# One list of steps from the first product on: the first half-slot of a quantised gated layer joins the ordered list, and the loads and weight ranges ahead of it are rearranged

## The chip, the core and the metric

The kernel runs on one core of one Trainium2 chip. Five engines work side by side, each through its own queue in order: TensorE (PE), VectorE (DVE), ScalarE (ACT), GpSimd (POOL) and SyncE (SP), which here issues nearly all DMAs. The metric is the device time in microseconds (us), as the median of the runs.

## The reference

For x of 4 x 1024 x 512 numbers, a condition of 4 x 128, norm_w (512 x 128), up_w (4096 x 512) and down_w (512 x 2048):

```
scale = cond @ norm_w.T + 1.0
ms = mean(x * x, axis=-1)
h = x * (scale[:, None, :] * rsqrt(ms + 1e-6))
u = h @ up_w.T
val, gate = split(u, 2)
h = val * gelu(gate)
y = act_quant(h) @ weight_quant(down_w).T
return y + x
```

act_quant rounds each token's row to 255 levels of its largest value, weight_quant rounds down_w to -1, 0, 1 times its mean size.

## The kernel before

The work goes in four batches of 1024 tokens, one for each row of the condition. The up product is cut into 16 blocks j of 128 value rows and 128 gate rows of up_w (the W blocks: t = 0 is the value half, t = 1 the gate half). Each factor is carried as two float16 numbers, a high part and a low part, and a product of two such numbers is made as three matmuls (high times high, and the two mixed ones). W rows and tokens are first scaled by powers of two, so that the parts fit.

In the first batch W has to be brought into that form while it is used. A block is loaded (w_load, line 310), its largest value is found (w_largest, 322: for blocks 0 to 2 by a reduce on DVE, from block 3 on by a sum on ACT), a power of two is made of it (w_factor_steps, 335), the rows are scaled by it (w_scale, 373, on POOL for blocks 0 and 1), PE turns 128 x 128 tiles into PSUM (w_turn, 382), ACT copies the high part out (w_high, 417) and DVE subtracts it for the low part (w_low, 426). Blocks 0 to 4 are multiplied plainly, in halves of 512 tokens: the steps gate, gelu, value and out (759 to 776), each of gate and value being 12 matmuls; the blocks after them run as slots (801), in which seven products serve for eight, and their parts go through DRAM: s_high, s_low and s_spill write them out (457 to 478).

x of the first batch needs, for each of its 8 tiles of 128 tokens, a sum of squares (first_sum, 1142), a root on ACT and a Newton step of five small DVE instructions for each pair of tiles (rsqrt_root, 1149; rsqrt_steps, 1155), a scaling (first_scale, 1169), four turns on PE (first_turn, 1176), a high part on ACT (first_high, 1181) and a low part on DVE (first_low, 1185), both multiplied by the condition's scale. That scale comes from cond: a row of the condition is spread over the partitions by PE (cond_first_row, 210), multiplied with norm_w on DVE (cond_scale, 216), its largest value found (cond_largest, 222), turned, reduced, floored to a power of two (cond_range_steps, 237), spread again (cond_spread, 256) and divided out (cond_undo, 262). The other three rows' scales come from small PE products with the turned norm_w (cond_turn, 191; cond_scale_rest, 201).

The order is written out by hand, and every engine takes its part of it in that order. It has three pieces. The first (1122 to 1260) issues the loads and brings four x tiles and block 0 into form; products of zeros (keep_warm, 1191) keep PE busy meanwhile. The second, plain_first (778), makes the 24 matmuls of block 0 with the first 512 tokens; two groups of other steps are put in between (second_part, 1263, ahead of matmul 6, and second_slot, 1291, ahead of matmul 16). The third is FIRST_BATCH (1380), a string of step names that take (1375) looks up in STEPS (1337) and issues one by one: all that is left of the first batch. In a name such as gate.1.0 the numbers are the step's arguments, here block 1 and half 0; slot.5.14 is the fifteenth step of block 5's slot, its value sum (856). Later batches are ordered by a planner with costs, which the change leaves as it is.

PSUM has eight banks: A and E two each, B one, po three. A tile that takes a bank waits until the one before it there has been read.

Of the kernel before, what the change touches and what calls it, by code (L numbers as in the profile page):

```python
# [51 lines left out]
def glu_quant_kernel(  # L52
# [138 lines left out]
    def cond_turn():  # L191

        pt = bank("E", 2, name="pc_t")
        PE.transpose(pt[:, :B], cn, ident[:B, :B])
        ACT.copy(cT, pt[:, :B])
        pt = bank("E", 2, name="nw_t")
        for k in range(NK):
            PE.transpose(pt[:, k * P : (k + 1) * P], nw[:, k], ident)
        ACT.copy(nwT, pt)
# [62 lines left out]
    def cond_undo(pd, b0, b1):  # L262
        DVE.reciprocal(ux[:, b0:b1], pd)
        if b0 == 0:
            DVE.tensor_scalar(scT[:, :, 0], scT[:, :, 0], ux[:, 0:1], None, ALU.mult)
# [512 lines left out]
    def plain_first(between):  # L778

        ps = {1: bank("B", 1, name="pg_0_0"), 0: bank("A", 2, name="pv_0_0")}  # L780
        gate, a21, a22 = a_parts(0)
# [4 lines left out]
        for n, (t, w, l, k) in enumerate(order):
            if n in between:
                between[n]()
            a = [gate[:, 0], gate[:, 1]] if t else [a21, a22]
# [1 line left out]
            PE.matmul(  # L791
                ps[t], a[:, w, k % 2, :], XP[:, l, k, :TOK],
                start=w + l + k == 0, stop=l == 1 and k == NK - 1,
            )
# [360 lines left out]
    def rsqrt_steps(n, m, z):  # L1155

        t, y = ssq0[:, n : n + m], rs0[:, n : n + m]
        ms = sm.tile([P, m], F32, name=f"mean_sq_{n}", bufs=1)
        DVE.reciprocal(y, z)
# [809 lines left out]
```

## Time and profile before

| | us |
|---|---|
| median of 3 runs | 710.73 (709.88 to 711.68) |
| the profiled execution | 710.89 |
| its span in the profile | 709.0 |
| around the span | 1.89 |

| engine | busy us | share of the span |
|---|---|---|
| PE, matmuls | 702.5 | 99% |
| DVE | 594.8 | 84% |
| ACT | 397.1 | 56% |
| POOL | 152.5 | 22% |

A line of a timeline has the start and the duration of an instruction (or of several alike, as x5), the engine, the line of the kernel, the operation, the tile written and the tiles read, and in brackets how long the engine had stood idle and what released it. Times are from the start of the span. A line of the waits names who waited, for whom, how long in all, how often, and the longest. A line of a table by stretches has the stretch, its length, the busy time and the number of instructions of PE, PE's weight loads, DVE, ACT and POOL, the share of its clock that PE was granted, the share of the DMA engines, and GB/s.

### The profile page before, as it was taken

The numbers are of one execution on the slowest core, as the hardware profiler recorded it, in microseconds if no ns is written. First come the engines' busy times: TensorE is split into PE (matmuls) and PEld (weight loads), VectorE is DVE, ScalarE is ACT, GpSimd is POOL, SyncE is SP. The second block draws the span as 40 slices with busy tenths as digits, with TensorE's granted clock in tenths as the row PEclk, the third lists the DMA queues.
The fourth block names the chain that finished last, engine by engine and source line by source line (L and its number), as shares of the span: only waits on it lengthen the run. The fifth ranks groups of instructions, "written<-read, shape, count | busy, mean of one in ns | idle before, by whom it ended". The sixth has DMA issues, their size and how long they took to land.

```text
span 709.0 us, 10268 instructions
## 1 busy us (share of the span) xinstructions
PE 702.5 (99%) x3668; PEld 359.8 (51%) x3668; DVE 594.8 (84%) x888; ACT 397.1 (56%) x692; POOL 152.5 (22%) x162
## 2 busy tenths in 40 slices
...
GB/s 259 323 268 253 249 198 260 218 207 226 272 131 167 178 178 165 140 178 210 133 113 110 133 106 171 178 183 148 219 104 97 99 103 103 101 100 99 77 223 104
DMA packets 223188, 120.26 MB, mean 170 GB/s; under 512 B 185353, under 2 KB 194589, under 8 KB 223138
## 3 DMA queue, kind: packets, MB, share of 16 engines
...
q10 hardware_dynamic: 152, 0.13, 0.1%
...
## 4 chain that ended last, share of the span: by engine, by line
PE 97%; DVE 1%; ACT 1%; DMA 1%; issue 0%; ACTq 0%; SPq 0%
PE A L703 43%; PE E L703 21%; PE B L703 11%; PE po L1071 9%; PE pg L718 3%; PE pv L718 3%; PE po_end L1018 2%; PE po_n L1071 2%; PE pz L1195 1%; DMA s_dram<-s_rows 1%; PE ptx L1179 1%; PE pv L791 0%; PE po_B L1071 0%; PE pg L791 0%; PE pw L388 0%; PE po_A L1071 0%
## 5 line engine op out<-in xcount | busy, mean ns | idle before, releaser
L703 PEld LDWEIGHTS <-SXY 128*128 128x128 f16 x2268 | 221.7, 98 | 260.7
L703 PE MATMUL A<-R,SXY 128*128 128x512 f16 x1170 | 270.7, 379 | 0.0
L703 PE MATMUL E<-R,SXY 128*128 128x512 f16 x606 | 147.2, 379 | 0.0
L840 DVE SCALAR_TENSOR_TENSOR H<-A,sg,t 128x512 f32<-128x512 f32 x59 | 44.2, 749 | 59.7 <-PE A L703 56.9
L851 ACT ACTIVATE t<-t,sg 128x512 f32<-128x512 f32 x59 | 42.5, 720 | 68.1 <-DVE t L848 67.9
L703 PE MATMUL B<-R,SXY 128*128 128x512 f16 x324 | 78.8, 379 | 0.0
L993 DVE TENSOR_TENSOR H<-H,am 128x1024 f32<-128x1024 f32 (+1 forms) x64 | 76.9, 1221 | 1.2 <-POOL am L962 1.2
L911 DVE TENSOR_REDUCE gm<-H 128x512 f32<-128x1024 f32 x56 | 69.2, 1236 | 1.0
L827 ACT COPY t<-A 128x512 f32<-128x512 f32 x59 | 34.4, 583 | 57.1 <-PE A L703 56.1
L927 POOL PARTITION_ALL_REDUCE am<-R x8 | 14.3, 1793 | 221.3 <-DVE R L913 221.3
L834 ACT ACTIVATE t<-B,sg 128x512 f32<-128x512 f32 x59 | 40.5, 686 | 37.7 <-PE B L703 37.7
L1071 PEld LDWEIGHTS <-R 128*128 128x128 bf16 (+1 forms) x512 | 50.1, 98 | 10.1
L857 DVE TENSOR_TENSOR v<-A,v 128x512 f32<-128x512 f32 x59 | 40.4, 684 | 15.1 <-PE A L703 12.5
L820 ACT COPY v<-E 128x512 f32<-128x512 f32 x59 | 34.5, 585 | 32.3 <-PE E L703 30.2
L1071 PE MATMUL po<-wd,R 128*128 128x256 fp8e4 x416 | 52.4, 273 | 0.0
L812 ACT COPY B<-A 128x512 f32<-128x512 f32 x59 | 33.8, 573 | 32.8 <-PE A L703 32.2
L860 DVE SCALAR_TENSOR_TENSOR H<-v,sg,t 128x512 f32<-128x512 f32 x59 | 45.8, 777 | 7.1 <-ACT t L851 6.7
L848 DVE TENSOR_TENSOR t<-E,t 128x512 f32<-128x512 f32 x59 | 39.9, 679 | 6.6 <-PE E L703 6.6
L913 DVE TENSOR_TENSOR R<-R,gm 128x512 f32<-128x512 f32 x56 | 41.7, 745 | 1.1
L1001 ACT CAST R<-H 128x1024 bf16<-128x1024 int32 x38 | 39.1, 1045 | 6.0 <-DVE H L993 5.6
L578 POOL TENSOR_SCALAR ssq<-ssq 128x2 f32<-128x2 f32 x12 | 5.5, 454 | 164.1 <-ACT xt L608 116.1
L703 PEld LDWEIGHTS <-R 128*128 128x128 f16 x210 | 20.5, 98 | 25.6 <-issue 0.9
...
## 6 DMA issues: line engine op xcount, KB each, us to landing
...
```

Source lines behind the costliest of these rows:

```text
L703: PE.matmul(o, s[:, w, k, :], operand(g // NJ, c, l, k), start=start and n == 0, stop=stop and n == len(TERMS) - 1, skip_group_check=True,)
L718: PE.matmul(ps, a[k // 2][:, w, k % 2, :], XP[:, l, k, h * TOK : (h + 1) * TOK], start=n == 0, stop=n == len(terms) - 1,)
L834: ACT.activation(self.t1, self.B, AF.Gelu, scale=gain(self.g, 1))
L840: DVE.scalar_tensor_tensor(h_half(self.g, 0), self.A, gain(self.g, 0), self.t1, ALU.mult, ALU.mult)
L848: DVE.tensor_tensor(self.t2, self.E, self.t2, ALU.add)
L851: ACT.activation(self.t2, self.t2, AF.Gelu, scale=gain(self.g, 1))
L857: DVE.tensor_tensor(self.v, self.A, self.v, ALU.add)
L860: DVE.scalar_tensor_tensor(h_half(self.g, 1), self.v, gain(self.g, 0), self.t2, ALU.mult, ALU.mult)
L911: DVE.tensor_reduce(gm[0], v, AX.X, ALU.max, apply_absolute_value=True)
L913: return [largest, lambda: DVE.tensor_tensor(m, m, gm[0], ALU.max)]
L993: DVE.tensor_tensor(v.bitcast(I32) if whole else v, v, r.to_broadcast([P, 2, TOK]), ALU.mult)
L1071: PE.matmul(po, w[:, j], m, start=start and j == 0, stop=stop and j == n - 1, skip_group_check=True,)
```

## The change

The work is the same but for small things; its order and its engines change.

- **Loads on SP:** x 0:2, then norm_w, x 2:4, W0, W1, x 4:6, x 6:8, W2. Before: norm_w, x 0:2, x 2:4, W0, x 4:6, x 6:8, W1, W2.
- **Ahead of the first product:** eleven products of zeros instead of sixteen. The first pair of x tiles is scaled, and tile 0 turned, before the second pair is squared; norm_w is turned early, and its copy on ACT stands behind the second root. The condition's largest is clamped by a fifth column of 1e-30 instead of an instruction, and the factor 1/256 is in the row that spreads it.
- **W0 and W1 are ranged by sums of absolute values:** three halves on ACT (half_sum), the value half of W0 on DVE (value_sum), each half with its own factor.
- **W0's gate half** is copied and split in two quarter-size pieces on DVE (gate_half) instead of one copy on ACT and one subtraction on DVE.
- **plain_first, second_part and second_slot are gone.** Their matmuls, turns, splits, squares and scalings are steps of FIRST_BATCH; x4 is scaled on POOL, its square is on ACT. The gate product takes a bank A and the value product a bank E; before it was B and A.
- **The rest of FIRST_BATCH** holds the same steps as before in another order.

```diff
     DVE.memset(unmagic, -MAGIC)
-    one = cpool.tile([P, 1], F32, name="one")
+    one = cpool.tile([P, 2], F32, name="one")
+    one, down_x = one[:, 0:1], one[:, 1:2]
     DVE.memset(one, 1.0)
+    DVE.memset(down_x, 1.0 / X_UP)
...
-    scT = cpool.tile([P, NK, B], F32, name="scT")
+    scT5 = cpool.tile([P, NK + 1, B], F32, name="scT")
+    scT = scT5[:, :NK]
+    DVE.memset(scT5[:, NK], 1e-30)
...
-    def cond_turn():
-        pt = bank("E", 2, name="pc_t")
+    def cond_turn(pt):
...
         ACT.copy(cT, pt[:, :B])
-        pt = bank("E", 2, name="nw_t")
+    def weight_turn(pt):
...
             PE.transpose(pt[:, k * P : (k + 1) * P], nw[:, k], ident)
+    def weight_copy(pt):
...
     def cond_largest(b0, b1):
-        v = scT[:, :, b0:b1]
         if b0 == 0:
+            v = scT[:, :, b0:b1]
             DVE.tensor_scalar(v, v, 1.0, None, ALU.add)
+        v = scT5[:, :, b0:b1]
...
         yield
-        DVE.tensor_scalar(d4, d4, 1e-30, None, ALU.max)
-        yield
...
         DVE.tensor_scalar(dg, ident[:n, :n], d4, 1.0 / X_UP, ALU.mult, ALU.mult)
+    def cond_range_one(pm):
+        d1 = sm.tile([B, 1], F32, name="d4_0", tag="d4")[:1]
+        DVE.tensor_reduce(d1, pm, AX.X, ALU.max)
+        yield d1
+        pow2_floor(d1)
+    def cond_undo_steps(pd):
+        DVE.reciprocal(ux[:, 0:1], pd)
+        yield
+        DVE.tensor_scalar(scT[:, :, 0], scT[:, :, 0], ux[:, 0:1], None, ALU.mult)
+        yield
+        DVE.tensor_copy(dx[:, 0:1], pd)
...
         DVE.reciprocal(ux[:, b0:b1], pd)
-        if b0 == 0:
-            DVE.tensor_scalar(scT[:, :, 0], scT[:, :, 0], ux[:, 0:1], None, ALU.mult)
...
         return am
+    def half_sum(j, t):
+        am = sm.tile([P, 2], F32, name=f"wam_{j}_{t}", tag="wam")[:, t : t + 1]
+        jk = junk[:, 2 * j].bitcast(F16)[:, :D]
+        ACT.activation(jk, wn(j)[:, t], AF.Abs, scale=0.5 / W_UP, accum_out=am)
+        return am
+    def value_sum():
+        am = sm.tile([P, 2], F32, name="wam_0_0", tag="wam")[:, 0:1]
+        DVE.tensor_reduce(am, wn(0)[:, 0], AX.X, ALU.add, apply_absolute_value=True)
+        return am
+    def half_factor_steps(j, t, am, u=1.0):
+        c = slice(t, t + 1)
+        pow2_floor(am)
+        yield
+        DVE.tensor_scalar(sw[:, j, c], am, u, 0.5 * 2.0**-100 / W_UP, ALU.mult, ALU.max)
+        yield
+        if j not in iv:
+            iv[j] = sm.tile([P, 2], F32, name=f"iv_{j}", tag="iv", bufs=3)
+        DVE.reciprocal(iv[j][:, c], sw[:, j, c])
...
             ACT.copy(a22[:, 0], v[:, 1])
+    def gate_half(n):
+        gate, _, _ = a_parts(0)
+        g = pw[0][0][:, n * HALF : (n + 1) * HALF]
+        DVE.tensor_copy(gate[:, n, 0], g)
+        DVE.tensor_tensor(gate[:, n, 1], g, gate[:, n, 0], ALU.subtract)
...
-    def plain_first(between):
...
+    PLAIN = [(1, w, 0, k) for w in range(2) for k in range(2)]
+    PLAIN += [(1, w, 0, k) for k in range(2, NK) for w in range(2)]
+    PLAIN += [(0, w, 0, k) for w in range(2) for k in range(NK)]
+    PLAIN += [(t, 0, 1, k) for k in range(NK) for t in (1, 0)]
+    def first_product(n):
+        t, w, l, k = PLAIN[n]
+        if w + l + k == 0:
+            halves[0, 0, t] = bank("A" if t else "E", 2, name=f"{'vg'[t]}_0_0")
         gate, a21, a22 = a_parts(0)
+        a = ([gate[:, 0], gate[:, 1]] if t else [a21, a22])[k // 2]
+        a = a.rearrange("p w (k f) -> p w k f", k=2)
+        PE.matmul(
+            halves[0, 0, t], a[:, w, k % 2, :], XP[:, l, k, :TOK],
+            start=w + l + k == 0, stop=l == 1 and k == NK - 1,
+        )
+    def first_gelu():
+        halves[0, 0] = wpool.tile([P, TOK], F32, name="g_0_0", tag="t1")
+        ACT.activation(halves[0, 0], halves[0, 0, 1], AF.Gelu, scale=gain(0, 1))
+    def first_out():
+        DVE.scalar_tensor_tensor(
+            h_half(0, 0), halves[0, 0, 0], gain(0, 0), halves[0, 0], ALU.mult, ALU.mult
+        )
...
     ACT.dma_start(out=cn, in_=cond)
-    SP.dma_start(out=nw, in_=norm_w.rearrange("(k p) c -> p k c", p=P))
-    ACT.activation(start_t, one, AF.Sqrt)
...
         ms = sm.tile([P, m], F32, name=f"mean_sq_{n}", bufs=1)
+        DVE.tensor_scalar(ms, t, 1.0 / D, EPS, ALU.mult, ALU.add)
+        yield
         DVE.reciprocal(y, z)
-        yield
-        DVE.tensor_scalar(ms, t, 1.0 / D, EPS, ALU.mult, ALU.add)
...
     first_load(0, 2)
+    SP.dma_start(out=nw, in_=norm_w.rearrange("(k p) c -> p k c", p=P))
+    ACT.activation(start_t, one, AF.Sqrt)
     first_load(2, 2)
     w_load(0)
+    w_load(1)
     first_load(4, 2)
     first_load(6, 2)
-    w_load(1)
     w_load(2)
-    keep_warm(3)
+    pz = bank("A", 2, name="pz")
+    keep_warm(3, pz)
     pc = cond_first_row()
-    keep_warm(5)
-    cond_scale(0, pc)
-    mx = cond_largest(0, 1)
-    pm = cond_over(mx, 0, 1, "A")
+    nw_t = bank("E", 2, name="nw_t")
+    few = bank("E", 2, name="cond_few")
+    pm, pd, ps = few[:1, :P], few[:, P : P + 1], few[:, 2 * P : 2 * P + NK * (B - 1)]
+    cond_turn(few)
+    keep_warm(4, pz)
     first_sum(0)
     first_sum(1, DVE)
     root = rsqrt_root(0, 2)
-    keep_warm(4)
-    cond_turn()
-    steps = cond_range_steps(pm, 0, 1)
-    dg = next(steps)
-    next(steps)
-    next(steps)
-    in_turn(rsqrt_steps(0, 2, root), steps)
-    pd = cond_spread(dg, 0, 1, "A")
-    ps = bank("E", 2, name="ps")[:, : NK * (B - 1)]
-    pz = bank("A", 2, name="pz")
-    for k in range(2):
-        cond_scale_rest(ps, (k,))
-        keep_warm(2, pz)
+    in_turn(rsqrt_steps(0, 2, root))
+    weight_turn(nw_t)
+    cond_scale(0, pc)
+    first_scale(0, ACT)
+    first_scale(1, ACT)
+    keep_warm(2, pz)
+    ptx = [po_bank(f"ptx_0_{k}") for k in range(3)] + [bank("A", 2, name="ptx_0_3")]
+    first_turn(0, ptx)
     first_sum(2)
     first_sum(3, DVE)
-    am = w_largest(0, 1, 2)
+    mx = cond_largest(0, 1)
+    PE.transpose(pm, mx, ident)
+    first_turn(1, ptx)
     root = rsqrt_root(2, 2)
-    factor = w_factor_steps(0, am, 1, 2)
-    in_turn(rsqrt_steps(2, 2, root), islice(factor, 2))
-    first_scale(0, ACT)
-    first_scale(1, ACT)
+    am = half_sum(0, 1)
+    factor = half_factor_steps(0, 1, am)
+    newton = rsqrt_steps(2, 2, root)
+    in_turn(islice(newton, 3))
+    steps = cond_range_one(pm)
+    dg = next(steps)
+    in_turn(newton, steps)
+    PE.matmul(pd, down_x[:1].to_broadcast([1, P]), dg, start=True, stop=True)
+    keep_warm(2, pz)
+    first_scale(2, ACT)
+    weight_copy(nw_t)
     in_turn(factor)
+    w_scale(0, (1,), POOL)
     first_scale(3, DVE)
-    first_scale(2, ACT)
-    w_scale(0, (1,))
-    cond_undo(pd, 0, 1)
...
+    in_turn(cond_undo_steps(pd))
+    first_turn(3, ptx)
+    v_am = value_sum()
+    first_turn(2, ptx)
+    w_turn(0, [bank("E", 2, name="pw_0_1"), bank("B", 1, name="pw_0_0")], (1,))
...
     }
-    def second_slot():
-        w_turn(1)
-        w_high(1)
-        first_scale(4, ACT)
-        first_scale(5, DVE)
-        w_low(1)
...
+    def keep_half(j, t):
+        made["am", j, t] = half_sum(j, t)
...
         "turn": next_turn,
-        "x_scale": lambda n: first_scale(n, ACT if n % 2 == 0 else DVE),
+        "first": first_product, "first_gelu": first_gelu, "first_out": first_out,
+        "x0_high": lambda k: first_high(0, k, ptx[k]), "x0_low": lambda k: first_low(0, k, ptx[k]),
+        "half": gate_half, "v_factor": lambda: in_turn(half_factor_steps(0, 0, v_am, 0.5 / W_UP)),
+        "w0_scale": lambda t: w_scale(0, (t,), POOL), "w1_scale": lambda t: w_scale(1, (t,), POOL), "w_turn": lambda j, t: w_turn(j, ts=(t,)),
+        "w_high": lambda j, t: w_high(j, (t,)), "w_low": lambda j, t: w_low(j, (t,)),
+        "w_sum": keep_half, "w_half": lambda j, t: in_turn(half_factor_steps(j, t, made["am", j, t])),
+        "x_sum": lambda n, e=0: first_sum(n, (ACT, DVE)[e]),
+        "x_root": lambda: rsqrt(ssq0[:, 4:8], rs0[:, 4:8], DVE),
+        "gelu_load": lambda: ACT.activation(start_t, neghalf[:, 0:1], AF.Gelu),
+        "c_rest": lambda k: cond_scale_rest(ps, (k,)),
+        "c_rest_copy": lambda: ACT.activation(
+            scT[:, :, 1:], ps.rearrange("p (k b) -> p k b", b=B - 1), AF.Copy, bias=1.0
+        ),
+        "x_scale": lambda n, e=0: first_scale(n, (ACT, DVE, POOL)[e]),
...
     FIRST_BATCH = """
-        x_scale.6 gate.1.0 turn.6 turn.5 x_scale.7 s_sum.0.0 gelu.1.0 s_sum.0.1.1 s_sum.0.2.1 turn.4 s_high.0.0
-        turn.7 x_high.0 x_high.3 o_whole.2.2.0 x_high.2 value.1.0 w_range.2 s_sum.0.3 w_factor.2 s_low.0.0.1
-        x_low.0 s_sum.1.0.1 d_load.7 t_load.0 s_high.0.1 w_load.11 s_sum.1.1 x_high.1 s_low.0.1 t_load.1 x_low.2
-        w_load.3 w_scale.2.0 x_low.1 o_whole.0.0.0 x_low.3 gate.0.1 w_load.10 d_load.6 w_range.3 out.1.0
-        w_load.9 w_scale.2.1 s_sum.1.2.1 rows_high.2 s_sum.1.3.1 s_high.1.1 w_factor.3 w_scale.3.0 s_high.1.0
...
-        slot.5.7 s_turn.6.1 s_sum.7.3 gelu.4.1 slot.5.10 s_high.7.1 max.1.1.0 w_gain.8 s_spill.6.2 rows_turn.7
...
+        v_factor w0_scale.0 x0_high.0 half.0 half.1 c_rest.2 x0_high.1 x0_high.3 c_rest.0 c_rest.1 x0_high.2 c_rest.3
+        w_gain.0 c_rest_copy first.0 first.1 w_turn.0.0 first.2 x0_low.0 first.3 first.4 w_sum.1.1 w_high.0.0 w_sum.1.0
+        w_half.1.1 w1_scale.1 w_low.0.0 w_half.1.0 first.5 first.6 x0_low.1 x0_low.2 x0_low.3 x_sum.4 x_sum.5 first.8
+        first.9 w1_scale.0 first.10 first.11 first.12 first.13 w_gain.1 first.14 w_turn.1.1 first.7 w_high.1.1 first.16
+        w_low.1.1 first.15 x_sum.7 x_sum.6 first.17 first.19 w_turn.1.0 first.18 w_high.1.0 first.21 x_root x_scale.4.2
+        x_scale.5.1 w_low.1.0 first.20 gelu_load first.22 first.23 first_gelu x_scale.7.1 first_out x_scale.6.0
+        gate.1.0 turn.5 s_sum.0.0 turn.4 gelu.1.0 s_sum.0.1.1 s_sum.0.2.1 turn.6 s_high.0.0 turn.7 x_high.0
+        o_whole.2.2.0 w_range.2 x_high.2 value.1.0 x_high.1 w_factor.2 x_high.3 s_sum.0.3 x_low.0 s_low.0.0.1 x_low.1
+        s_high.0.1 x_low.2 s_sum.1.1 d_load.7 t_load.0 w_load.11 w_load.3 s_low.0.1 c_rows w_range.3 o_whole.0.0.0
+        t_load.1 x_low.3 w_load.10 gate.0.1 s_sum.1.0.1 out.1.0 d_load.6 w_scale.2.0 w_scale.2.1 s_sum.1.2.1
...
+        o_WHOLE.1.0.1 w_scale.4.0 rows_low.3 out.0.1 w_scale.4.1 c_store gelu.1.1 w_gain.2 w_load.9 gate.2.0
...
+        s_high.7.0 rows_low.7 s_low.7.0 w_scale.8.1 s_spill.4.0 w_scale.8.0 rows_high.8 slot.5.7 s_turn.6.1 out.4.0
+        s_high.7.1 gelu.4.1 slot.5.10 slot.5.14 max.1.1.0 w_gain.8 s_spill.6.2 rows_turn.7 slot.6.1 slot.5.11 slot.5.8
...
     """
-    plain_first({6: second_part, 16: second_slot})
     take(FIRST_BATCH)
```

More of the change, by code (lines that the diff above doesn't have):

```diff
@@ L1234, in glu_quant_kernel @@
+    factor = half_factor_steps(0, 1, am)
[8 more added lines that the diff above has]
+    weight_copy(nw_t)
     in_turn(factor)
+    w_scale(0, (1,), POOL)
     first_scale(3, DVE)
-    first_scale(2, ACT)
-    w_scale(0, (1,))
-    cond_undo(pd, 0, 1)
-    ptx = [po_bank(f"ptx_0_{k}") for k in range(3)] + [bank("A", 2, name="ptx_0_3")]
@@ L1240, in glu_quant_kernel @@
-    for n in (0, 1, 3, 2):
-        first_turn(n, ptx)
-    w_turn(0, [bank("E", 2, name=f"pw_0_{t}") for t in (1, 0)], (1,))
-    cond_scale_rest(ps, (2, 3))
-    w_range(0, 0, 1)
-    first_high(0, 0, ptx[0])
-    w_high(0, (1,))
-    ACT.activation(
-        scT[:, :, 1:], ps.rearrange("p (k b) -> p k b", b=B - 1), AF.Copy, bias=1.0
-    )
-    w_scale(0, (0,))
-    first_sum(4, DVE)
-    w_low(0, (1,))
-    w_gain(0)
-    first_high(0, 1, ptx[1])
-    first_high(0, 2, ptx[2])
-    first_high(0, 3, ptx[3])
@@ L1257, in glu_quant_kernel @@
-    first_sum(5)
-    w_range(1)
-    w_gain(1)
-    w_scale(1, (0,))
-    first_low(0, 0, ptx[0])
-    def second_part():
-        w_turn(0, ts=(0,))
-        w_high(0, (0,))
-        w_low(0, (0,))
-        w_scale(1, (1,))
-        first_sum(6)
-        first_sum(7)
-        first_low(0, 1, ptx[1])
-        first_low(0, 2, ptx[2])
-        rsqrt(ssq0[:, 4:8], rs0[:, 4:8], DVE)
-        first_low(0, 3, ptx[3])
-        ACT.activation(start_t, neghalf[:, 0:1], AF.Gelu)
+    in_turn(cond_undo_steps(pd))
@@ L1396, in glu_quant_kernel @@
-        o_sum.2 w_load.7 o_sum.3 s_low.4.0.1 w_factor.6 w_scale.6.1 s_sum.5.0.1 s_sum.5.2.1 s_sum.5.3
-        s_spill.4.2 s_spill.5.1 s_high.5.0 s_low.5.0 out.2.1 max.0.1.0 slot.5.0 s_spill.4.1 s_turn.5.0 gelu.3.1
-        value.3.1 slot.5.2 w_scale.6.0 rows_high.6 out.3.0 s_sum.6.0.1 o_high.2 s_sum.5.1 s_high.5.1 d_sum.7
-        rows_low.6 o_low.2 s_spill.5.0 slot.5.1 slot.5.6 out.3.1 w_load.8 rows_turn.6 s_sum.6.2.1 w_range.7
-        s_low.5.1.1 s_sum.6.1.1 s_turn.5.1 slot.5.3 s_high.6.0 o_high.0 value.4.0 c_undo gelu.4.0 c_bring
@@ new lines, in glu_quant_kernel @@
+        rows_low.4 w_range.5 s_spill.3.1 s_high.2.1 s_high.2.0 out.1.1 s_low.2.0.1 s_spill.2.0 o_high.1 s_sum.3.0.1
+        gelu.2.0 w_factor.5 s_sum.3.2 s_sum.3.1.1 s_high.3.0 w_load.14 s_low.2.1 o_low.1 s_sum.3.3 w_scale.5.0
+        s_low.3.0.1 s_sum.4.0.1 w_scale.5.1 s_high.3.1 rows_turn.4 w_load.6 gate.3.0 rows_high.5 out.2.0 rows_low.5
+        gelu.2.1 value.2.1 w_load.13 c_over s_low.3.1.1 value.3.0 c_range c_spread gate.4.0 o_high.3 o_low.3 gate.3.1
+        s_spill.3.0 gate.4.1 w_gain.4 gelu.3.0 d_sum.6 s_sum.4.2 s_sum.4.3.1 s_high.4.1 w_range.6 s_sum.4.1 max.0.0.0
```

131 lines of the change are left out of this document (54 added, 77 removed).

## The prediction

> **What bounds the kernel now.** I read the page first, then the waits of TensorE (PE), then the timelines of the first 32 us, engine by engine.
>
> ```profile
> span 709.0 us, 10268 instructions
> PE 702.5 (99%) x3668; PEld 359.8 (51%) x3668; DVE 594.8 (84%) x888; ACT 397.1 (56%) x692; POOL 152.5 (22%) x162
> PE 97%; DVE 1%; ACT 1%; DMA 1%; issue 0%; ACTq 0%; SPq 0%
> ```
>
> PE is busy for 99% of the span and carries 97% of the chain that ended last. The products and turns that the change touches are the same in number, so time can only come from the start, before PE runs without a gap, or from a wait of PE later on. The waits of PE show one after the start:
>
> ```profile
> PE A L703 <- DVE v L857: 0.7, 1, 0.7
> ```
>
> The start itself, on PE:
>
> ```profile
> 3.66 2.31 PE L1195 MATMUL pz<-H 128*128 128x512 f16 x5
> 9.76 0.59 PE L1195 MATMUL pz<-H 128*128 128x512 f16 x2
> 14.34 0.39 PE L791 MATMUL pg<-R,SXY 128*128 128x512 f16 x1 [0.34 <-ACT SXY L421]
> 14.99 1.24 PE L791 MATMUL pg<-R,SXY 128*128 128x512 f16 x5 [0.27 <-ACT R L1183]
> 16.07 0.60 PE L388 MATMUL pw<-ident,H 128*128 128x128 f32 x4
> 21.47 2.79 PE L718 MATMUL pg<-R,SXY 128*128 128x512 f16 x12
> ```
>
> The first real product is at 14.34 us; from 14.99 on PE is all but full. I take the start of gate.1.0 at 21.47 as the mark: behind it stands the same PE work in both kernels. Before 14 us PE only warms up (L1195) and turns tiles, so dropping five of the sixteen warm-up products is worth nothing by itself; the loads and VectorE (DVE) set the time:
>
> ```profile
> 8.54 0.69 DVE L1147 SCALAR_TENSOR_TENSOR R<-H 128x512 f32<-128x512 f32 x1 [0.36 <-DMA H<-in_x_dram]
> 10.45 0.17 DVE L1159 RECIPROCAL rs<-newton 128x2 f32<-128x2 f32 x1 [0.58 <-ACT newton L1152]
> 11.16 0.16 DVE L1167 SCALAR_TENSOR_TENSOR rs<-newton,rs 128x2 f32<-128x2 f32 x1
> 11.36 0.49 DVE L1174 TENSOR_SCALAR H<-H,rs 128x512 f32<-128x512 f32 x1
> 11.96 0.48 DVE L265 TENSOR_SCALAR scT<-scT,ux 128x4 f32<-128x4 f32 x1
> 12.40 0.67 DVE L332 TENSOR_REDUCE wam<-H 128x1 f32<-128x512 f32 x1
> 13.11 0.16 DVE L171 TENSOR_TENSOR wam<-wam,undo 128x1 int32<-128x1 int32 x1
> 13.50 0.16 DVE L348 RECIPROCAL iv<-sw 128x1 f32<-128x1 f32 x1
> 14.99 1.21 DVE L332 TENSOR_REDUCE wam<-H 128x2 f32<-128x1024 f32 x1
> 17.43 0.42 DVE L432 TENSOR_TENSOR R<-pw,R 128x256 f16<-128x256 f32 x1
> 18.09 1.40 DVE L1187 SCALAR_TENSOR_TENSOR R<-ptx,scT,R 128x512 f16<-128x512 f32 x2
> 30.25 0.74 DVE L776 SCALAR_TENSOR_TENSOR H<-pv,sg,g 128x512 f32<-128x512 f32 x1
> ```
>
> The second pair of x tiles lands at 8.54, and DVE then works almost in one piece to 13.66.
>
> **The change, part by part.** *Loads.* SyncE's queue now issues x 0:2, norm_w, x 2:4, W0, W1, x 4:8. Ahead of the landing at 8.54 stand the same three loads, so I keep 8.54. The first x pair lands earlier, which is worth nothing here: its two tiles are scaled while the second pair is still out. norm_w lands later, and the dot products of the condition (cond_scale) with it; they now run after the first pair's Newton step, still ahead of 8.54. x 4:8 come one W block later; their squares now start at about 16.8, well behind.
>
> *From the landing to the first turn of W0's value half.* ScalarE (ACT) and GpSimd (POOL) have these rows:
>
> ```profile
> 8.88 0.58 ACT L199 COPY R<-nw_t 128x512 f32<-128x512 f32 x1 [0.59 <-PE nw_t L198]
> 10.12 0.29 ACT L1152 ACTIVATE newton<-ssq,eps 128x2 f32<-128x2 f32 x1
> 14.25 1.85 ACT L1183 ACTIVATE R<-ptx,scT 128x512 f16<-128x512 f32 x3
> 18.60 1.28 ACT L1274 ACT_TABLE_LOAD   x1
> 28.93 0.64 ACT L328 ACTIVATE H<-H 128x512 f16<-128x512 f32 x1
> ```
> ```profile
> 13.76 1.05 POOL L380 TENSOR_SCALAR H<-H,iv 128x512 f32<-128x512 f32 x1 [1.34 <-DMA H<-in_L_cond_up_w_dram]
> 19.65 1.06 POOL L579 TENSOR_TENSOR rs<-ssq,neghalf 128x4 f32<-128x4 f32 x1 [1.41 <-DVE ssq L578]
> ```
>
> The copy of the turned norm_w (8.88) moves behind the root, so ACT takes the square of x2 at 8.54 instead of after it, and the root is there at about 9.65 instead of 10.41. DVE squares x3 until 9.2, takes the condition's largest by two small steps (0.2 each, the spacing of the rows 13.11 to 13.50) until 9.6, and starts the reciprocal at 9.75 instead of 10.45: 0.7 earlier. Most of that is spent again. The five Newton instructions (10.45 to 11.32 before, with W0's factor between them) now hold one small reduce of the condition's largest, put at 0.3, and its floor to a power of two; its clamp is gone (a fifth column does it) and its 1/256 went into PE's broadcast. They end at 10.65; W0's factor follows by itself, three steps, 0.55, until 11.25. Scaling x3 starts at 11.25 against 11.36. The gate half of W0 is now ranged by a sum on ACT, beside all this. Then as before: scaling 0.4, undoing the condition's scale 0.65 (the 0.48 of row 11.96 in it; between 0.17 for its size and 0.48, I take the measured one), the value half's sum 0.67, its factor 0.55: 13.55. POOL scales the value half in about 1.0 (row 13.76: 1.05) and PE can turn it at 14.55. In between, DVE splits the gate half by two quarter-size copies and two subtractions, 0.33 apart by row 17.43 (the row has no such copy; between 0.2 and 0.42); the first gives product 0 at 14.0 and product 1 at 14.2.
>
> *The first half-slot.* From that turn on I let PE run full: three groups of four turns, 0.44 each (row 16.07: 0.60 less the overlap), and 22 products at 0.2165 (row 14.99: (1.24-0.38)/4), 1.32 + 4.76 = 6.08. gate.1.0 starts at **20.63 against 21.47, a gain of 0.84**. What must keep pace: ACT's four high parts of x, 0.58 apart by row 14.25, begin once PE has turned x2 (12.5) and run until 14.95; one sum of W1 (0.61, the spacing of the two sums at row 28.93 on) and the value half's high parts end at 16.0, product 8 wants them at 16.07. DVE's low parts of the value half end at 16.85, product 12 wants them at 16.95. These two have no slack: whatever either is late is lost one for one. x's low parts (0.67 apart, row 18.09) end at 19.8, wanted at 20.2.
>
> *Work moved between engines.* DVE loses a half reduce (0.67), the reduce of W1 (1.21) and one square (0.7), and gains the gate's two copies, 0.65. ACT gains three sums and a square, about 2.5, and loses the gate's high copy and a scaling, about 1.2. The Gelu table load (18.60 before) moves behind squares and W1's high parts to about 20.75, the first Gelu to 22.1; PE wants its bank back at 23.2 for the next x turns, so 0.4 of cover is left. POOL's power (1.06) ends at 21.7 and it then scales x4 until 22.6, ahead of turn.4 at 23.7. Behind these two on POOL stands block 0's first sum, which feeds only a spill, and on SyncE's queue no load waits for a moved step before 14 us. DVE waits for that power for 1.2, so by out.1.0 (row 30.25) it is level with before while PE is 0.84 ahead.
>
> *The later list.* The one late wait of PE:
>
> ```profile
> 66.82 0.75 DVE L776 SCALAR_TENSOR_TENSOR H<-pv,sg,g 128x512 f32<-128x512 f32 x1 [0.74 <-PE pv L718]
> 74.34 0.62 ACT L459 CAST s_rows<-H 128x512 f16<-128x512 f32 x1 [2.08 <-DMA s_dram<-s_rows]
> 78.50 1.24 DVE L911 TENSOR_REDUCE gm<-H 128x512 f32<-128x1024 f32 x1
> 79.67 0.67 DVE L857 TENSOR_TENSOR v<-A,v 128x512 f32<-128x512 f32 x1
> ```
>
> ACT waits 2.08 for a spill to leave its buffer, DVE's queue behind it is late, and the value sum at 79.67 holds PE until 80.4. The new list puts that sum ahead of the reduce at 78.50 but behind out.4.0 (which stood at 74.53): 1.17 - 0.7 = 0.47 earlier. Ahead of the spill, DVE waited 0.74 for PE (row 66.82); with PE ahead this shrinks by 0 to 0.74, as the DMA queues let it. PE goes on at 79.2 to 79.9 instead of 80.4: a gain of 0.5 to 1.2, whatever it had at 21 us. I take 0.9, near the middle. Later no wait is seen in before; for the rest of the new order I take nothing, with bounds of 0.5 either way.
>
> **Sum.** The profiled execution took 710.89 (span 709.0 and 1.89 around it): 710.89 - 0.9 = 710.0. The median of the runs shown, 710.73, lies 0.16 lower, so 709.8.
>
> **Rivals.** *A larger gain.* The landing at 8.54 is the lever of the whole start: if the new order of loads brings it 1 us earlier, and the spill chain follows, the gain is 0.84 + 1 + 0.66 = 2.5: 708.3. For it: nothing but that wait keeps DVE from starting. Against: the same bytes stand ahead.
>
> *The clock drops.* PE now idles from about 7.8 to 9.6, and products at half speed are 0.43 apart (row 3.66) against 0.22 (row 9.76). Three stretches, the first two 3.41 long:
>
> ```profile
> 8.42:11.83 3.41, 2.89 (x19) 1.80 (x18) 2.64 (x13) 2.92 (x7) 0.32 (x1) 1.00 1.05 404
> 704.74:708.15 3.41, 1.14 (x11) 0.78 (x8) 0.72 (x2) 0.00 (x0) 0.00 (x0) 1.00 0.51 192
> 708.15:709.00 0.85, 0.00 (x0) 0.00 (x0) 0.00 (x0) 0.00 (x0) 0.00 (x0) 0.50 0.00 0
> ```
>
> A stretch with 2.89 of 3.41 busy kept the clock; one with 1.14 busy was followed by 0.50. After the change the stretch from 8.42 would hold about 1.7, between the two. If the clock falls, the twelve turns up to 13.1 and the first products run at half speed until the next busy stretch ends near 15.2: about 0.9 later, which eats the gain: 710.7. The Trainium skill (TensorE: Matmul & The Clock Gate, "Part 1: The HAM clock gate") has the clock fall only after an idle window of about 3.4 us; by that rule a stretch half busy keeps it and the sum stands. The last two rows do not quite agree: a third busy was not enough.
>
> *Slower: the spill chain moves back.* The new list issues the 512 KB loads of W9 and W13 later, W9 from behind out.1.0 to behind gelu.1.1, W13 from before value.1.1 to behind value.2.1, so nearer to the spill.
>
> ```profile
> 50.00:60.00 10.00, 10.00 (x49) 4.57 (x48) 9.31 (x16) 6.13 (x13) 2.58 (x3) 1.00 0.81 196
> 70.00:80.00 10.00, 9.73 (x46) 4.31 (x44) 8.37 (x17) 7.89 (x17) 4.72 (x5) 1.00 1.03 239
> ```
>
> At 70 to 80 the DMA engines are full; 512 KB more at 239 GB/s is 2.2 us. If both loads push on the spill, ACT's 2.08 becomes up to 6.5, and PE, having no more than 1 us of cover there, waits about 3.3 more: 710.0 + 3.3 = 713.3. It decides once the spill lands over 1 us later than in before. Against it: 50 to 60 has 19% free, 1.9 us, which takes one of them whole.
>
> **How the numbers follow.** A difference under 0.3% (2.1 us) is what a measurement of this kernel cannot tell from none. Forecast 0.45, larger gain 0.2, clock 0.2, spill chain 0.15. Under 708.6 lies most of the larger gain and a little of the forecast: 0.2. Over 712.9 lies most of the spill case: 0.13. The rest, 0.67, is no change. The range runs from 707.5 to 712.6: it holds the forecast and the clock case, the larger gain down to its middle and some more, and leaves out most of the spill case.
>
> **What would show it.** Right: gate.1.0 near 20.6, no PE wait from 14.55 on, DVE's square of x3 still starting at 8.5, PE's wait at the value sum shorter than 0.66. Wrong: products 0.43 apart after 12 us (clock), a landing of the second x pair at 7.5 or 9.5, a PE wait of over 0.3 at product 8 or 12, or an ACT wait for the spill longer than 2.08.

## The result, and the profile after

The kernel after the change took 718.84 us in the median of 4 runs (717.33 to 721.20), beside 710.62 for the kernel before on the same chip (4 runs, 709.88 to 711.68): a ratio of 1.0117, with an interval of 1.0083 to 1.0152. It is slower by 8.2 us, where 709.8 and at most 712.6 were forecast. The profiled execution was the longest of the four, 721.2.

The page of after: span, busy times, and the shares of the chain that ended last.

```profile
span 719.3 us, 10273 instructions
PE 705.8 (98%) x3663; PEld 362.0 (50%) x3663; DVE 604.4 (84%) x889; ACT 399.1 (55%) x698; POOL 158.6 (22%) x163
PE 83%; DVE 9%; ACT 3%; issue 2%; DMA 2%; POOL 1%; SPq 0%; DVEq 0%; ACTq 0%; POOLq 0%
```

PE has the same work, but only 83% of the chain instead of 97%; DVE has 9% instead of 1%. And DVE is busy for 604.4 us instead of 594.8, with one instruction more: about 10 us of DVE time came up without work behind it.

The table by stretches shows where PE lost. The columns after the length are PE, weight loads, DVE, ACT and POOL. First before, then after:

```profile
22.00:36.00 14.00, 14.00 (x75) 7.26 (x73) 13.69 (x28) 12.52 (x25) 6.05 (x5) 1.00 0.88 303
36.00:100.00 64.00, 63.34 (x295) 28.65 (x293) 56.74 (x99) 53.68 (x106) 29.14 (x31) 1.00 0.96 249
100.00:165.00 65.00, 65.00 (x303) 29.45 (x302) 57.55 (x94) 53.09 (x107) 33.35 (x38) 1.00 0.97 219
```
```profile
22.00:36.00 14.00, 13.16 (x69) 6.66 (x67) 12.51 (x20) 11.02 (x22) 9.19 (x8) 1.00 0.61 225
36.00:100.00 64.00, 60.13 (x276) 26.56 (x275) 60.98 (x99) 51.33 (x98) 29.53 (x28) 1.00 0.94 243
100.00:165.00 65.00, 63.41 (x292) 28.28 (x291) 56.13 (x91) 53.85 (x113) 33.05 (x36) 1.00 1.00 223
```

Count PE's instructions: 6, 19 and 11 fewer, 36 in all. At the 0.2165 of a product that is 7.8 us. Between 36 and 100 us DVE does as many instructions as before, 99, in 60.98 us instead of 56.74, and is 95% busy.

The start, on PE, and two stretches of the same table, both of the profiled execution of after:

```profile
14.83 1.01 PE L834 MATMUL g<-R,SXY 128*128 128x512 f16 x2
22.74 2.75 PE L761 MATMUL pg<-R,SXY 128*128 128x512 f16 x12
30.61 0.28 PE L287 MATMUL pr<-ident,scT 128*16 128x128 f32 x1 [0.77 <-DVE R L1234]
42.42 2.76 PE L761 MATMUL pg<-R 128*128 128x512 f16 x12 [0.83 <-DMA R<-H]
46.22 2.75 PE L761 MATMUL pv<-R 128*128 128x512 f16 x12 [1.03 <-DVE H L819]
```
```profile
7.52:10.93 3.41, 2.17 (x13) 1.19 (x13) 2.75 (x17) 2.66 (x7) 0.41 (x1) 1.00 1.05 397
10.93:14.34 3.41, 3.41 (x18) 3.41 (x18) 2.29 (x9) 2.49 (x5) 1.04 (x2) 0.50 0.74 281
```

gate.1.0 starts at 22.74, 1.27 later than before: in this execution the clock fell to half from 10.93 to 17.76, after a stretch in which PE was busy for 2.17 of 3.41 us. That and the 7.8 make 9.1 of the 10.3 us between the two profiled executions; some records are missing from the count (3663 against 3668). From 30 us on PE waits again and again, mostly for DVE, where before it had one such wait of 0.7.

Now DVE beside POOL in the stretch behind the start. Before (DVE, then POOL):

```profile
21.62 0.68 DVE L430 TENSOR_TENSOR SXY<-pw,SXY 128x512 f16<-128x512 f32 x1
23.94 0.75 DVE L442 TENSOR_TENSOR H<-H 128x256 f32<-128x256 f32 x2
```
```profile
21.38 2.30 POOL L727 TENSOR_TENSOR H<-R 128x1024 f32<-128x1024 f16 x1
```

After, the same steps:

```profile
26.16 2.02 DVE L485 TENSOR_TENSOR H<-H 128x256 f32<-128x256 f32 x2
33.31 1.98 DVE L485 TENSOR_TENSOR H<-H 128x256 f32<-128x256 f32 x1
35.21 0.74 DVE L819 SCALAR_TENSOR_TENSOR H<-pv,sg,g 128x512 f32<-128x512 f32 x1
```
```profile
25.26 2.30 POOL L770 TENSOR_TENSOR H<-R 128x1024 f32<-128x1024 f16 x1
32.88 2.13 POOL L770 TENSOR_TENSOR H<-R 128x1024 f32<-128x1024 f16 x1
```

These are sums of W's quarters (s_sum), both inputs in SBUF. Two of them took 0.75 before, and take 2.02 after; one alone takes 1.98. In each case POOL's o_whole, which reads SBUF for over 2 us, began before them, and they end 0.3 to 0.6 after it. In before, o_whole ran beside subtractions that take one input from PSUM, and neither grew. out.1.0 starts on DVE at 35.21 instead of 30.25.

### The profile page after: what moved, and what is told of

Its sections match the earlier page's. It is cut to its first block, busy times and chain, and to the rows that moved or that the text cites. A ratio compares the mean times of both kernels' runs of the same rounds, so it can differ in the third digit from the quotient of the medians.

```text
span 719.3 us, 10273 instructions
## 1 busy us (share of the span) xinstructions
PE 705.8 (98%) x3663; PEld 362.0 (50%) x3663; DVE 604.4 (84%) x889; ACT 399.1 (55%) x698; POOL 158.6 (22%) x163
## 4 chain that ended last, share of the span: by engine, by line
PE 83%; DVE 9%; ACT 3%; issue 2%; DMA 2%; POOL 1%; SPq 0%; DVEq 0%; ACTq 0%; POOLq 0%
PE A L746 39%; PE E L746 19%; PE B L746 10%; PE po L1120 9%; PE po_end L1067 2%; PE po_n L1120 2%; DVE H L485 2%; DMA H<-in_x_dram 1%; DVE SXY L506 1%; ACT H L415 1%; DVE H L445 1%; DMA SXY<-H 1%; DVE gm L960 1%; DVE wd L779 1%; DMA H<-in_L_cond_up_w_dram 1%
## 5 line engine op out<-in xcount | busy, mean ns | idle before, releaser
L962 DVE TENSOR_TENSOR R<-R,gm 128x512 f32<-128x512 f32 x56 | 40.2, 718 | 1.1
```

The source lines that it names most:

```text
L962: return [largest, lambda: DVE.tensor_tensor(m, m, gm[0], ALU.max)]
```

## The experiments

Theories at the outset: **A**, the loss has two parts, the clock that fell at the start and a DVE held up from 25 us on; **B**, it is the clock alone; **C**, it is the rest of the new order alone. Out of the traces came, for the rest of the order, **D**: a DVE instruction with two inputs in SBUF is held while a POOL instruction that reads SBUF is under way; the new order puts such pairs side by side, and DVE, all but full to 100 us, then holds PE. And **E**: the new order's own dependencies and queues hold PE, whatever POOL does. Ratios are to the kernel before in the same call. "New list" means FIRST_BATCH from gate.1.0 on.

**e1_warm: the clock kept.**

```diff
     first_turn(0, ptx)
+    keep_warm(4, pz)
...
     first_turn(1, ptx)
+    keep_warm(1, pz)
```

> The changed kernel with five more products of zeros: four behind the first x tile's turn, one behind the second's. Theory A (the loss has two parts, the clock at half speed from 10.9 to 17.8 us and VectorE held up from 25 us on): the granted clock stays at 1.00 from about 8 us on, gate.1.0 starts at 20.5 to 21.5, and the time falls by 1 to 3 us against the profiled 721.2 of the changed kernel, to 717 to 719. Theory B (the clock alone): back to 711 or under. Theory C (the new order of the later list alone): no change, 718 to 721.

720.76 (720.06 to 721.97), ratio 1.0145 (1.0128 to 1.0162). The clock is full from 5.1 us on, and PE is 1.80 ahead of before at gate.1.0:

```profile
19.67 2.75 PE L761 MATMUL pg<-R,SXY 128*128 128x512 f16 x12
43.18 2.75 PE L761 MATMUL pv<-R 128*128 128x512 f16 x12 [1.04 <-DVE H L819]
```

Yet the kernel is no faster than after: the time is C's, and A's 717 to 719 is missed too. B falls: e3 below has the same list behind the old start, gate.1.0 at 21.38 and the same value product at 42.77, so a lead of 1.71 at 20 us is gone by 43. The start by itself, with the clock kept, is 1 us better than the 20.63 forecast in this execution.

**e2_old_tail and e3_new_tail: one half of the change each.** e2 has the new start and, from gate.1.0 on, the old list; e3 has the old start and the new list.

```diff
 e2: ... first_gelu first_out
-x_scale.6.0 gate.1.0 turn.5 s_sum.0.0 turn.4 gelu.1.0 s_sum.0.1.1 s_sum.0.2.1 ...
+x_scale.6.0 gate.1.0 turn.6 turn.5 x_scale.7.1 s_sum.0.0 gelu.1.0 s_sum.0.1.1 s_sum.0.2.1 ...
 e3: plain_first({6: second_part, 16: second_slot})
-x_scale.6 gate.1.0 turn.6 turn.5 x_scale.7 s_sum.0.0 gelu.1.0 s_sum.0.1.1 s_sum.0.2.1 ...
+x_scale.6 x_scale.7 gate.1.0 turn.5 s_sum.0.0 turn.4 gelu.1.0 s_sum.0.1.1 s_sum.0.2.1 ...
```

> The changed kernel up to gate.1.0, and from there the list in the order of before. Theory A: GpSimd's first large sum of x still lies beside VectorE's two sums of W0, so VectorE still loses 1.3 us there, but the second collision and the early c_rows are gone: 714 to 717. Theory C (the later list's new order): 711 or under. Theory B: 718 to 721.

> The kernel of before up to gate.1.0, and from there the list in the new order. Theory A: VectorE is ahead by 2.6 us at the first output, so the collisions shift; at most the c_rows wait (0.8 us) and one collision (1.5 us) are left: 711 to 713.5. Theory C: 716 or more, most of the loss with the old start. Theory B (clock alone): 710 to 711.

e2: 712.13 (710.94 to 716.54, 10 runs), ratio 1.0027 (1.0009 to 1.0045). e3: 720.79 (719.72 to 722.41), ratio 1.0142 (1.0125 to 1.0159). The new list by itself makes the whole loss: e3 is C's figure (716 or more), not A's (711 to 713.5). e2 lies between C's 711 and A's 714, and most of its 1.4 goes with the clock: the five runs with a mean clock of 1.00 took 710.94 to 711.63, the five below that 712.62 to 716.54. The waits of PE in e3, and DVE and POOL at the same place as above:

```profile
PE A L703 <- DVE v L857: 2.9, 5, 1.3
PE A L703 <- DMA SXY<-H: 2.0, 1, 2.0
PE pv L718 <- DVE H L776: 1.5, 2, 1.0
PE A L703 <- DVE H L840: 0.7, 1, 0.7
PE A L703 <- ACT t L827: 0.5, 1, 0.5
```
```profile
29.86 1.97 DVE L442 TENSOR_TENSOR H<-H 128x256 f32<-128x256 f32 x1
31.76 0.74 DVE L776 SCALAR_TENSOR_TENSOR H<-pv,sg,g 128x512 f32<-128x512 f32 x1
```
```profile
29.43 2.13 POOL L727 TENSOR_TENSOR H<-R 128x1024 f32<-128x1024 f16 x1
```

POOL reads until 31.56; the sum, alone 0.41, ends at 31.83. Only then comes out.1.0, at 31.76 instead of 30.25. DVE is busy for 606.6 us in e3.

**e4_pool: three steps moved apart in after.**

```diff
-... x0_low.3 x_sum.4 ... x_high.0 o_whole.2.2.0 w_range.2 ... s_low.0.0.1 x_low.1 ...
+... x0_low.3 o_whole.2.2.0 x_sum.4 ... x_high.0 w_range.2 ... s_low.0.0.1 s_sum.1.0.1 x_low.1 ...
-... s_sum.1.1 d_load.7 ... w_range.3 o_whole.0.0.0 ... gate.0.1 s_sum.1.0.1 out.1.0 ...
+... s_sum.1.1 o_whole.0.0.0 d_load.7 ... w_range.3 ... gate.0.1 out.1.0 ...
```

> The changed kernel with three steps moved in the list: GpSimd's two large sums of x (o_whole.2.2.0 to behind x0_low.3, o_whole.0.0.0 to behind s_sum.1.1) so that they run beside VectorE work that reads PSUM, and s_sum.1.0.1 back ahead of x_low.1. Theory A: the four sums of W parts on VectorE go back from 1.12 us in the mean to 0.45, 2.7 us in all, and the time falls by 2 to 3 us, to 715 to 718. Theory B or C: within 1 us of the changed kernel, since VectorE's duration is not what PE waits for.

722.02 (720.92 to 724.88), ratio 1.0163 (1.0140 to 1.0187). The edit was a poor one: o_whole.2.2.0 now stands ahead of w1_scale.0 on POOL, PE waits 2.0 for W1's scaled half, and the clock falls from 26.2 to 29.6. Neither expected figure is met, and it decides nothing.

**e5_one_step: one pair of steps moved apart in e3.**

```diff
-s_low.0.0.1 x_low.1 ... gate.0.1 s_sum.1.0.1 out.1.0
+s_low.0.0.1 s_sum.1.0.1 x_low.1 ... gate.0.1 out.1.0
```

> The kernel of before up to gate.1.0, then the new order (as e3_new_tail), with one step moved: s_sum.1.0.1 back to behind s_low.0.0.1. Theory D (the new order puts VectorE's instructions that read two SBUF tiles beside GpSimd's, and they are held until GpSimd is done): that sum takes 0.42 us instead of 1.97, PE's wait of 1.05 at 42.8 us is gone, and the time falls by about 1.0 to 1.3 from 720.8, to 719.5 to 719.8. Theory E (the new order is late by its dependencies and by SyncE's queue): within 0.3 us of 720.8.

719.57 (718.75 to 720.47), ratio 1.0124 (1.0108 to 1.0139). The moved sum on DVE, and PE's waits for out (DVE H L776), 1.5 in e3:

```profile
27.05 0.42 DVE L442 TENSOR_TENSOR H<-H 128x256 f32<-128x256 f32 x1
```
```profile
PE pv L718 <- DVE H L776: 0.8, 2, 0.4
```

The sum takes 0.42 instead of 1.97, and out.1.0 starts 8.95 behind gate.1.0 (29.37 and 20.42) instead of 10.38, as D has it. PE's wait of 1.05 is 0.38 and not gone; the next two sums now meet o_whole and take 1.57 (0.94 in before). The time is in D's range, 1.2 us under e3, but by the ratios it is 0.9, and their intervals overlap; so the trace bears D out here, and the time alone does not.

**e6_warm_old_tail: the new start at its best.** The edits of e1 and e2 together.

> The new start with the five more products of zeros of e1_warm, then the list in the order of before. In e1_warm PE was 1.8 us ahead of before at 25 us. If that is kept: 708.5 to 709.5. If the spill's wait near 80 us takes it back, as the prediction feared: 710 to 711. If the loss had come with the new start after all: over 712.

711.42 (710.60 to 712.45, 11 runs), ratio 1.0012 (1.0004 to 1.0021). gate.1.0 starts at 18.87, 2.60 ahead of before, and PE then waits 0.79 and 0.69 for DVE and ACT at 24 and 28 us, and 0.71 at the value sum. The time lies between the second figure expected and the third: the lead is not kept. The first of these waits comes from this pair of DVE and POOL, in which DVE's instruction has one input only:

```profile
21.62 2.23 DVE L1221 TENSOR_SCALAR H<-H,rs 128x512 f32<-128x512 f32 x1
```
```profile
21.45 2.12 POOL L770 TENSOR_TENSOR H<-R 128x1024 f32<-128x1024 f16 x1
```

In before the same scaling, begun when o_whole has 0.14 to go, takes 0.47 us:

```profile
23.54 0.47 DVE L1174 TENSOR_SCALAR H<-H,rs 128x512 f32<-128x512 f32 x1
```

**e7_more_read and e8_more_set: the disputed cost by itself.** The kernel before, with 23 instructions more on POOL that nobody waits for, at the same places; in e7 they read SBUF, in e8 they only write it.

```diff
+    def pool_more():
+        d = junk[:, 0]
+        POOL.tensor_tensor(d[:, :HALF], d[:, :HALF], d[:, HALF:], ALU.subtract)   # e7
+        POOL.memset(d, 1.0)                                                       # e8
...
-s_sum.1.0.1 ... s_sum.1.1 ...
+s_sum.1.0.1 more ... s_sum.1.1 more ...      (behind each such s_sum and s_low of blocks 1 to 8)
```

> The kernel of before with 23 more GpSimd instructions in the first batch's list, each reading two SBUF tiles of 128x256 and depending on nothing (one behind each GpSimd sum or low part of blocks 1 to 8, about 0.73 us each, 17 us in all). Theory D: VectorE's two-input instructions are held beside them, up to 0.7 us each, and PE's waits grow: 713 to 719. Theory E: within 1 us of the kernel before, the same as e8_more_set, since GpSimd is idle three quarters of the time.

> As e7_more_read, but each of the 23 instructions only writes (a memset of 128x512), with no SBUF read. Theory D in its narrow form (only a GpSimd instruction that reads holds VectorE): 710.5 to 711.5. If any GpSimd instruction holds VectorE, or if GpSimd's queue is what counts: the same as e7_more_read for equal durations.

e7: 718.35 (718.23 to 718.61), ratio 1.0111 (1.0097 to 1.0125). e8: 710.85 (710.06 to 711.52, 10 runs), ratio 1.0006 (0.9997 to 1.0015). The line of busy times of e7, then of e8:

```profile
PE 703.5 (98%) x3668; PEld 359.6 (50%) x3668; DVE 606.2 (85%) x888; ACT 397.7 (55%) x692; POOL 179.1 (25%) x185
```
```profile
PE 702.3 (99%) x3668; PEld 359.7 (51%) x3668; DVE 597.5 (84%) x888; ACT 397.4 (56%) x692; POOL 165.1 (23%) x185
```

23 readers on POOL, with nothing added to DVE, make DVE's 888 instructions 11.4 us longer (594.8 to 606.2) and the kernel 7.9 us; 23 writers make them 2.7 longer (why is not shown) and the kernel not slower by its interval. The readers also take twice as long on POOL (26.6 us in all against 12.6). One of PE's new waits in e7, 2.3 us for a spilled part, comes by way of POOL, but POOL had stood idle for 3.33 us when it began that part's sum at 64.29 (61.10 in before). The sum follows this scaling on ACT, which waited for DVE's factor and came 3.2 later than in before (60.28):

```profile
63.47 0.72 ACT L378 ACTIVATE H<-H,iv 128x512 f32<-128x512 f32 x1 [2.98 <-DVE iv L348]
```

So this wait goes back to DVE as well; the reader that stands on POOL between the sum and the part's low half adds 0.7 of its own.

**e9_before_set and e10_new_tail_set: POOL's reading taken out of both orders.** The kernel before, and e3, with the same edit:

```diff
-        eng.tensor_tensor(sf[:, o], m, l, op)
+        k = slice(0, HALF)
+        if eng is POOL:
+            POOL.memset(sf[:, o], 0.5)
+            k = slice(0, 16)
+        eng.tensor_tensor(sf[:, o, k], m[:, k], l[:, k], op)
...                                     (the same in s_low and t0_whole)
```

> The kernel before, with every first-batch subtraction and addition of GpSimd that reads whole tiles (s_sum, s_low, o_whole) replaced by a fill of the same output, which reads nothing, and the same operation on 16 columns only, which keeps the waits. The products then work with wrong numbers; their count is the same. It is the base for the next kernel. Theory D (a VectorE instruction with two inputs in SBUF is held while GpSimd reads SBUF): VectorE has less work by the stretch of its sums before, some 5 to 10 us less busy, but TensorE had no wait to lose but one of 0.7: 709.8 to 710.8. Theory E (the new order's own dependencies): the same.

> The kernel with the new later list behind the old start (720.79 when it was run), with the same replacement. Theory D: what VectorE lost by the meeting with GpSimd comes back. What is left over the kernel before with the replacement is TensorE's one wait for a DMA of about 2.0 near 100 us and 0.5 to 1 of others: 712 to 714. Theory E: the waits are between steps, whatever GpSimd reads: about 10 over the kernel before with the replacement, 719 to 721.

e9: 710.88 (710.09 to 711.36, 10 runs), ratio 1.0000 (0.9991 to 1.0009). e10: 712.92 (711.61 to 714.06, 6 runs), ratio 1.0030 (1.0019 to 1.0042). In e9 DVE is busy for 7.5 us less than in before (587.3) and no time is gained: PE had only its wait of 0.7 to lose there. The new list's loss falls from 10.0 us to 2.0 when POOL hardly reads. Most of what is left on PE in e10:

```profile
103.90 2.67 PE L711 MATMUL A<-R,SXY 128*128 128x512 f16 x6 [2.09 <-DMA SXY<-H]
```

It is the wait for a DMA that e3 has too, and behind it six products take 2.67 us instead of 1.46: the clock fell in that wait, in this execution. So E has a part, of about 2 us, and POOL's reading the other 8. Behind the start, PE's waits for DVE are 5.6 us in e3 and 0.7 in e10. POOL's own lateness is hardly seen in e3: its waits from 19 to 170 us show none of PE for POOL, one of DVE, the 0.5 for POOL's power that before has too, and 4.0 us of ACT instead of 2.7. The groups of W's sums on DVE (line, count, busy time and mean ns of one) from 22 to 165 us, in before, e9, e3, e10 and after:

```profile
L442 DVE TENSOR_TENSOR H<-H 128x256 f32<-128x256 f32 x25 | 11.1, 445 | 1.5 <-issue 0.9
```
```profile
L446 DVE TENSOR_TENSOR H<-H 128x256 f32<-128x256 f32 x25 | 10.4, 419 | 1.6 <-POOL H L444 0.9
```
```profile
L442 DVE TENSOR_TENSOR H<-H 128x256 f32<-128x256 f32 x25 | 15.9, 641 | 0.6
```
```profile
L446 DVE TENSOR_TENSOR H<-H 128x256 f32<-128x256 f32 x25 | 10.4, 419 | 2.8 <-POOL H L444 2.2
```
```profile
L485 DVE TENSOR_TENSOR H<-H 128x256 f32<-128x256 f32 x25 | 16.4, 658 | 0.6
```

The same 25 instructions: 419 ns each in both orders when POOL does not read, 445 in the old order, 641 and 658 in the new one.

**e11_mix_start and e12_mix_both: can the parts beat the kernel before?** e11 is e6 with DVE's held scaling on ScalarE and a copy moved out of the way; e12 also takes the value sum ahead of the reduce, the one later gain that the prediction named.

```diff
-x_scale.6.0 gate.1.0 turn.6 turn.5 x_scale.7.1 s_sum.0.0 ... turn.4 s_high.0.0 turn.7 x_high.0 x_high.3 o_whole.2.2.0 x_high.2
+x_scale.6.0 gate.1.0 turn.6 turn.5 x_scale.7.0 s_sum.0.0 ... turn.4 turn.7 x_high.0 x_high.3 o_whole.2.2.0 x_high.2 s_high.0.0
 e12 as well:
-s_high.7.1 max.1.1.0 w_gain.8 s_spill.6.2 rows_turn.7 slot.6.1 slot.5.14 max.1.1.1
+s_high.7.1 slot.5.14 max.1.1.0 w_gain.8 s_spill.6.2 rows_turn.7 slot.6.1 max.1.1.1
```

> The new start with its extra warm-up products and the old later list (711.42 when it was run), with x_scale.7 on ScalarE instead of VectorE, where it took 2.2 us beside GpSimd's o_whole, and s_high.0.0 behind the high parts of x. Theory D: TensorE's waits of 0.8 and 0.7 at 24 and 28 us go, and it keeps the 1.5 that the start gained; with the wait of 0.7 at the value sum still there, some of that is waited off again: 709.5 to 710.5, about 0.5 under the kernel before. Rival (VectorE has no slack to 80 us, so whatever TensorE gains by then is given back at the value sum): 710.7 to 711.4.

> The same, and the value sum of block 5's slot (slot.5.14) ahead of VectorE's reduce of 1.2 us (max.1.1.0) in the later list: the step of the prediction that was to take TensorE's one late wait away, by itself. Theory D: 0.7 under the kernel without it, 709.0 to 710.0. Rival (VectorE's queue waits on the spill, so TensorE waits for the sum whatever stands ahead of it): no change against the kernel without it.

e11: 710.83 (710.35 to 712.00, 11 runs), ratio 1.0003 (0.9994 to 1.0011): 0.6 under e6 (the intervals overlap), no better than before: the rival's figure, not D's. e12: 711.45 (710.90 to 712.54, 11 runs), ratio 1.0010 (1.0001 to 1.0019): no gain over e11 (the intervals overlap). D's 709.0 to 710.0 fails; the time is the rival's, but not for its reason. PE and DVE's t in e11, then in e12:

```profile
19.82 2.75 PE L761 MATMUL pg<-R,SXY 128*128 128x512 f16 x12
30.23 3.83 PE L761 MATMUL pg<-R,SXY 128*128 128x512 f16 x17 [1.06 <-DVE R L1234]
80.87 1.46 PE L746 MATMUL A<-wd,R 128*128 128x512 f16 x6 [0.84 <-DVE v L906]
81.33 0.68 DVE L897 TENSOR_TENSOR t<-E,t 128x512 f32<-128x512 f32 x1
```
```profile
79.39 1.46 PE L746 MATMUL A<-wd,R 128*128 128x512 f16 x6
82.19 1.46 PE L746 MATMUL E<-wd,SXY 128*128 128x512 f16 x6 [1.34 <-DVE t L897]
81.46 0.68 DVE L897 TENSOR_TENSOR t<-E,t 128x512 f32<-128x512 f32 x1
```

In e11 PE starts 1.65 ahead of before (19.82 against 21.47) and waits it off: 0.41 for ACT at 27.7, 1.06 for the low parts of x at 30.2, 0.84 at the value sum, 2.31 in all, where before has its 0.66: the difference is the whole lead. In e12 the value sum holds nobody, and PE waits 1.34 for the next thing that it needs from DVE, t. That stands behind the reduce in either order and comes no earlier. Of the steps ahead of it, the one with two inputs in SBUF at line 962 now runs beside a POOL sum and takes 1.17 instead of 0.68.

## Why the prediction was wrong, point by point

- **The step that failed** is the last of the sum: "for the rest of the new order I take nothing, with bounds of 0.5 either way". It measures 10.0 us (e3, with the old start). About 8.0 of it goes when POOL hardly reads (e3 less e10): DVE held by a reading POOL. About 2 is left then (e10 less e9), most of it the wait for a DMA near 105 us. A list whose steps were only shuffled was taken to be worth what it was worth before; no pair of engines was laid side by side, and the fill of DVE was not weighed: the row from 50 to 60 us that the prediction shows has DVE busy for 9.31 of 10 and was read for its DMA share alone. At the place in question:

```profile
20.00:50.00 30.00, 30.00 (x149) 14.55 (x148) 28.97 (x52) 26.37 (x52) 13.44 (x13) 1.00 0.92 305
```

  DVE is busy for 28.97 of 30 us. That PE has no wait there does not show slack in DVE: leads and small growth are lost in it (e11; e8, with 2.7 us more on DVE spread out and no time lost), while this wait of e3 fell to 0.38 when one sum of 1.97 us was brought back to 0.42 (e5):

```profile
42.77 2.75 PE L718 MATMUL pv<-R 128*128 128x512 f16 x12 [1.05 <-DVE H L776]
```

- **"Level with before" by out.1.0** failed by the same cause. DVE is there at 35.21 instead of 30.25. Of these 4.96, 2.8 are there when POOL's power comes (22.45 instead of 19.65, as the profiled start was slow). From there on the sums beside o_whole grow by about 2.7 (2.02 for 0.75, 1.98 for 0.51), of which the rest of the stretch makes up some 0.6.
- **The start** was right in kind. The square of x3 did not start at 8.5 but at 7.93:

```profile
7.93 0.69 DVE L1194 SCALAR_TENSOR_TENSOR R<-H 128x512 f32<-128x512 f32 x1 [0.69 <-DMA H<-in_x_dram]
```

  "Ahead of the landing at 8.54 stand the same three loads, so I keep 8.54" is 0.6 off here, but the landing scatters by as much: this square starts at 7.17 to 8.54 in the profiled executions of the new start, its like at 7.87 to 8.96 in those of the old. With the clock kept, gate.1.0 starts at 19.67 in e1, 1.80 ahead of before. Over all profiled executions it is 18.87 to 19.82 (e1, e6, e11, e12) against 20.23 to 21.47 (before, e3, e5, e7 to e10), before being the latest; the means are 1.5 apart, where 0.84 was forecast.
- **"710.89 - 0.9"**, the gain carried to the end, failed too. A lead of 1.65 at 20 us is worth nothing at 81 (e11), since DVE comes no earlier: its value sum starts at 80.13, in before at 79.67.
- **The late wait** at the value sum was seen rightly, its removal not: "0.47 earlier" counted the reduce only as something ahead of the sum, and not that PE needs t next, which stands behind the reduce in either order (e12).
- **The rival of the clock** took place in the profiled execution: 2.17 of 3.41 busy, 0.5 after it. The other three runs of after had a mean clock of 1.00 and took 717.33 to 719.98. The Trainium skill (TensorE: Matmul & The Clock Gate, "Part 1: The HAM clock gate") has the clock fall only after an idle window; this trace does not agree, since a stretch 64% busy was enough. More than half of that busy time is turns (the rows of PE there); whether they count like products no run here tests. Its price was larger than the 0.9 given: gate.1.0 at 22.74 against 19.67 in e1. But it is not the loss of after (e1).
- **The slower rival** named the wrong mechanism. In after, ACT's late copy to the spill buffer waits for DVE and not for the spill, and from 19 to 170 us no wait of ACT for a DMA out of that buffer is over 1.1:

```profile
79.17 0.62 ACT L502 CAST s_rows<-H 128x512 f16<-128x512 f32 x1 [1.25 <-DVE xn L667]
```

- **Not settled**: after itself was not run with POOL's reading taken out, so the 8 and 2 are the new list's behind the old start; and what part of e7's 7.9 and of e10's return is POOL's own lateness is not measured, though the waits show little of it. After (718.84) is 1.9 faster than e1 and e3, in spite of the worst start; the intervals overlap, and in the profiled executions the wait for a DMA near 108 us is 0.35 in after and 1.97 in both others. What sets that wait is open.
